# A four-layer macaron network on one core: layer 2's expert stage taken chunk by chunk, and the mixers' constants made in layer 1

## The chip, the cores and the metric

The kernel runs on one core of a Trainium2 chip. The metric is the device time of one execution in microseconds (us). A core has five engines with a queue each: TensorE (PE in the profile, with PEld for the loading of the stationary operand), VectorE (DVE), ScalarE (ACT), GpSimd (POOL) and SyncE (SP), which here only issues loads and stores. They share SBUF, of which a tile takes so many bytes in each of 128 partitions, and PSUM, eight banks into which TensorE writes.

## What is computed

The input x has 2 rows of 512 tokens with 256 features. Four layers follow, each a half-weighted feed-forward part, a mixer, and the same half-weighted feed-forward part again:

```python
x = x + 0.5 * ffn(layernorm(x))
x = x + mixer(layernorm(x))
x = x + 0.5 * ffn(layernorm(x))
```

All of it is in float32. Layer 0 has a mixture of 32 experts of which 6 are taken, around retention attention. Layer 1 has a product with a binarized weight, around attention over the most important tokens. Layer 2 has an expert stage in which the best of 8 experts is taken, around a Mamba-2 mixer with 8 heads. Layer 3 has a mixture of 8 experts of which 2 are taken, around a Mamba-2 mixer with 64 heads. The feed-forward part of layer 2, which the change rewrites, is:

```python
logits = xt @ wg                                  # xt: normalized tokens, wg: 256 x 8
probs = softmax(logits)
idx = argmax(probs)                               # the first of equal ones
gate = probs[idx]
expert_out = einsum('nh,eoh->neo', xt, W) + b     # 8 experts, 256 x 256 each
out = einsum('ne,neo->no', onehot(idx) * gate, expert_out)
```

## The kernel before

**Tiling.** The 1024 tokens lie in SBUF as 8 chunks of 128 (`self.x`, NC = 8), four (CB = 4) to a row; a chunk has its tokens on the partitions. A product over the 256 features is two matmuls of 128 (KD = 2), each of which the profile lists as two instructions. To bring the features onto the partitions, a normalized chunk is transposed on TensorE with the identity, into PSUM, and copied back by DVE or ACT.

**Order of the work.** The stages are traced in the order of `STAGES`: `l0_ffn, l0_attn, l0_ffn, l1, l2_ffn, l2_attn, l2_ffn, l3_ffn, l3_attn, l3_ffn`. Around the stages of a layer stands its `..._weights` context (L2: `l2_weights`; L3: `l3_weights`). The framework then decides the order of the instructions in each engine's queue by a planner with modelled costs: an engine takes what the plan finds ready, so that a later stage's instruction may stand before an earlier one's. In parts of the mixers the order of the queues is fixed by hand (`in_order`).

**Buffers.** SBUF and PSUM buffers come from pools that are opened and closed like brackets and laid one behind the other; a pool that is opened after another was closed takes its place. Layer 1 (`l1`) has one SBUF pool `a1` with all its buffers, PSUM pool `a1s` (banks 0 to 3: the scores), and in banks 4 to 7 first `a1m` and then `a1n`. `l2_ffn` takes all eight banks for one pool, `f2m`; the mixer of layer 2 takes all eight again (`psM` 3, `psA` 5), and so does `moe`, which layer 3 begins with.

**Layer 1's end.** `l1` has a loop of 25 steps in which, per chunk, the attention (`scores`, `turn`, `values`, `finish`, `project`) and the second feed-forward part (`front`, `turn_x`, `back`) follow each other two steps apart. The last step adds the last chunk's product to x (L1163).

**Layer 2's constants and weights.** `l2_weights` first calls `mixer_constants` for the L2 mixer: small loads of the convolution's weights and three vectors (L1537 to L1543), a memset on DVE (L1539), seven transposes (L1549, L1551) and the copies L1544 and L1552, in pools of their own that are closed at once. Then it loads the experts' weights and transposes them: 32 matmuls (L1470) in PSUM pool `f2pm` with four banks, and eight copies to `w8T`, by DVE (L130) and ACT (L132) in turn. `l3_weights` does for the L3 mixer what `mixer_constants` did for that of L2, between layer 2's second feed-forward part and layer 3.

**Layer 2's feed-forward part.** `l2_ffn` goes by whole steps over all 8 chunks: `layernorm_T` measures (L208, L209), takes the inverse deviation on POOL (L217, L218), normalizes (L223) and transposes each row (L177, copies L130 and L132) into one buffer `xT` of 8192 bytes a partition; `logits` makes the routing products of all chunks (L317, copy L320); twelve DVE and ACT instructions on 128x64 tiles give each token's weight for each expert (L1492 to L1503); `comb_transposed` transposes these (L402, two copies); and then, for each chunk, the biases' product (L1509, addition L1510) comes first, then 16 matmuls for the 8 experts (L1514), whose results DVE adds into x, weighted, one expert at a time (L1519).

**The mixer of layer 2.** `mamba` begins with a `layernorm_T` of its own: pool `xT` (8192 bytes a partition), then pool `ln`. Its first row goes through `measure` (four chunks' moments, then one pair of POOL instructions), `norm` (four times L223) and `turn` (transposes L177); then the products `pd` (L1616) and the convolutions `pp` (L1675). It reads the constants from `self.mix`.

Of the kernel before, what the change touches and what calls it, by code (L numbers as in the profile page):

```python
# [10 lines left out]
F32 = mybir.dt.float32  # L11
# [7 lines left out]
P = 128  # L19
# [64 lines left out]
class Net:  # L84
# [650 lines left out]

    @contextmanager
    def l3_weights(self):
        self.mixer_constants("L3_attn_", 64)
        yield


# [358 lines left out]
    def l1(self):  # L1100
# [18 lines left out]
        NG = NH // NQ  # L1119
        with ExitStack() as es:  # L1120
            sb = es.enter_context(tc.tile_pool(name="a1", bufs=1))
            psS = es.enter_context(tc.tile_pool(name="a1s", bufs=1, space=PSUM))

            score = psS.tile([P, NQ, 2, 2, P], F32, name="ps_s")
            wi, bq, bk, bv, bo, bi = self.l1v
            wib = sb.tile([P, KD, P], F32, name="wib")
            bqs = sb.tile([P, KD], F32, name="bqs")
            xn = sb.tile([P, NC, D], F32, name="xn")
            xT = sb.tile([P, KD, T], F32, name="xT")
            qT = sb.tile([P, KD, T], F32, name="qT")  # L1130
# [3 lines left out]
            mask = sb.tile([P, NC], F32, name="mask")  # L1134
            place = sb.tile([P, NC, P], F32, name="place")
            mx = sb.tile([P, NC, NH], F32, name="mx")
# [39 lines left out]
            def importance(b):  # L1176

                bs = slice(b * CB, (b + 1) * CB)
                pb = psM.tile([P, S], F32, tag="mm", name="pb")
                for k in range(KD):  # L1180
                    nc.tensor.matmul(
                        pb, wib[:, k, :], xT[:, k, b * S : (b + 1) * S], start=(k == 0), stop=(k == KD - 1)
                    )
                ibs[b] = sb.tile([P, S], F32, tag="ib", name="ib", bufs=2)
                nc.vector.tensor_scalar(ibs[b], pb, bi, None, ALU.add)
                own = sb.tile([P, CB, P], F32, tag="cmp", name="own", bufs=4)
                nc.vector.tensor_tensor(
                    own,
                    ibs[b].rearrange("p (c t) -> p c t", c=CB),
                    self.ident.unsqueeze(1).to_broadcast([P, CB, P]),  # L1190
                    ALU.mult,
                )
                nc.vector.tensor_reduce(imp[:, bs], own, AX.X, ALU.add)

            def ranks(b, cc):
                c = b * CB + cc
                me, ib = imp[:, c : c + 1], ibs[b]
                t = sb.tile([P, S], F32, tag="cmp", name="cmp", bufs=4)
# [4 lines left out]
                t = sb.tile([P, S], F32, tag="cmp", name="cmp2", bufs=4)  # L1203
                at = S - P - cc * P
# [36 lines left out]
            def compact(b):  # L1241
# [16 lines left out]
                xk = sb.tile([P, KD + 1, P], F32, tag="xk", name="xk", bufs=2)  # L1258
                nc.vector.tensor_copy(xk, px)
                return xk  # L1260

            def keys(b, xk):
                used = xk[:, KD, :]
                pk = psM.tile([P, KD, P], F32, tag="mm", name="pk")
                for m in range(KD):
                    for k in range(KD):
# [6 lines left out]
                        )  # L1273
                kT = sb.tile([P, KD, P], F32, tag="kT", name="kT", bufs=2)
                for m in range(KD):
# [5 lines left out]
            def vals(b, xk):  # L1281
                kept = sb.tile([P, 1], F32, tag="kept", name="kept", bufs=2)
                nc.vector.tensor_reduce(kept, xk[:, KD, :], AX.X, ALU.add)
                uc = sb.tile([P, 1], F32, tag="uc", name="uc", bufs=2)
# [4 lines left out]
                vt = sb.tile([P, D], F32, tag="vt", name="vt", bufs=2)  # L1289
                nc.vector.tensor_tensor(vt, pv, bv, ALU.add)  # L1290
                nc.vector.tensor_scalar(
                    vas[b][:, :, 0:DH], vt.rearrange("p (h d) -> p h d", h=NH), uc, None, ALU.mult
                )


            with tc.tile_pool(name="a1m", bufs=4, space=PSUM) as psM:
                for c in range(NC + 4):
                    if c < NC:
                        front(c)
                    if c == CB:  # L1300
                        wt = self.w("w4")[:, : KD * 4 * D].rearrange("p (k n d) -> p k n d", k=KD, n=4)
# [146 lines left out]
    def l2_weights(self):  # L1448
# [29 lines left out]

    def l2_ffn(self):
        nc, tc = self.nc, self.tc  # L1480
        E = 8
        with ExitStack() as es:
            psM = es.enter_context(tc.tile_pool(name="f2m", bufs=8, space=PSUM))
            xT, row, measure, norm, turn = self.layernorm_T(es, psM)
            for b in range(B):
                row(b)
            sb = es.enter_context(tc.tile_pool(name="f2", bufs=1))
            lg = self.logits(sb, psM, xT, self.wg8, E)
            m = sb.tile([P, NC], F32, name="m")
            oh = sb.tile([P, NC, E], F32, name="oh")  # L1490
            bc = m.unsqueeze(2).to_broadcast([P, NC, E])
            nc.vector.tensor_reduce(m, lg, AX.X, ALU.max)  # L1492
            nc.vector.tensor_tensor(oh, lg, bc, ALU.is_equal)
            nc.vector.tensor_tensor(lg, lg, bc, ALU.subtract)
            nc.scalar.activation(lg, lg, AF.Exp)

            nc.vector.tensor_tensor(oh, oh, self.c["desc"].unsqueeze(1).to_broadcast([P, NC, E]), ALU.mult)
            nc.vector.tensor_reduce(m, oh, AX.X, ALU.max)
            nc.vector.tensor_tensor(oh, oh, bc, ALU.is_equal)
            nc.vector.tensor_reduce(m, lg, AX.X, ALU.add)  # L1500
            nc.vector.reciprocal(m, m)
            nc.vector.tensor_tensor(lg, lg, bc, ALU.mult)
            nc.vector.scalar_tensor_tensor(lg, lg, 0.5, oh, ALU.mult, ALU.mult)  # L1503
            combT = self.comb_transposed(sb, psM, lg, 1)
            for c in range(NC):
                cs = slice(c * P, (c + 1) * P)
                xc = self.x[:, c, :]
                pb = psM.tile([P, D], F32, tag="mm", name="pb")
                nc.tensor.matmul(pb, combT[:, 0, cs], self.b8, start=True, stop=True)  # L1509
                nc.vector.tensor_tensor(xc, xc, pb, ALU.add)  # L1510
                for e2 in range(E // 2):
                    ps = psM.tile([P, 2, D], F32, tag="mm", name="ps_y")
                    for k in range(KD):
                        nc.tensor.matmul(  # L1514
                            ps, xT[:, k, cs], self.w8T[:, k, 2 * e2 : 2 * e2 + 2, :], start=(k == 0), stop=(k == KD - 1)
                        )
                    for e in range(2):
                        ei = 2 * e2 + e
                        nc.vector.scalar_tensor_tensor(  # L1519
                            xc, ps[:, e, :], lg[:, c, ei : ei + 1], xc, ALU.mult, ALU.add  # L1520
                        )


    def mixer_constants(self, pre, nh):

        nc, tc, a = self.nc, self.tc, self.a
        NX = nh * 64 // P
# [4 lines left out]
        cols = self.keep.tile([P, 7, R], F32, name=pre + "cols")  # L1534
        with tc.tile_pool(name=pre + "c", bufs=1) as sb, tc.tile_pool(name=pre + "cp", bufs=1, space=PSUM) as ps:
            cw = sb.tile([R, P, 4], F32, name="cwr")
            nc.sync.dma_start(cw, a[pre + "conv_w"].rearrange("(m p) w -> m p w", p=P))  # L1537
            v = sb.tile([R, 3, P], F32, name="vr")
            nc.vector.memset(v, 0.0)  # L1539
            nc.sync.dma_start(v[:, 0, :], a[pre + "conv_b"].rearrange("(m p) -> m p", p=P))  # L1540
            nc.sync.dma_start(v[:NX, 1, :], a[pre + "norm_w"].rearrange("(m p) -> m p", p=P))
            d = sb.tile([NX, 2], F32, name="dr")
            nc.sync.dma_start(d, a[pre + "D_param"].rearrange("(m two) -> m two", two=2))  # L1543
# [3 lines left out]
            pt = ps.tile([P, 7, R], F32, name="pt_c")  # L1547
            for w in range(4):
# [3 lines left out]
            nc.vector.tensor_copy(cols, pt)  # L1552
        self.mix = cols[:, 0:4, :], cols[:, 4, :], cols[:, 5, :], cols[:, 6, :], prm

# [7 lines left out]
    def mamba(self, pre, win, wout, nh):  # L1562
# [14 lines left out]
        with ExitStack() as es:  # L1577
# [7 lines left out]
            wb, self.wb = self.wb, None  # L1585
            cw, cb, nw, dcol, prm = self.mix
            cw = cw.rearrange("p w m -> p m w")
# [531 lines left out]
```

## Time and profile before

| | us |
|---|---|
| median of 3 runs (2030.21 to 2033.29) | 2031.36 |
| the profiled execution: its time | 2029.85 |
| its span, from first to last instruction | 2028.0 |
| PE busy | 1762.7 (87% of the span) |
| DVE busy | 1131.6 (56%) |
| POOL busy | 903.5 (45%) |
| ACT busy | 800.6 (39%) |
| granted TensorE clock, mean | 0.917 |

Times inside the profile are counted from the span's start, so 852.70 means 852.70 us after the first instruction. The profiled execution's own time is 1.85 us more than its span; the median of the runs is 1.51 us more than the profiled time. A busy PE is not a PE at its peak, because matmuls overlap: what one costs is best read from the distance between the starts of two. The granted clock is a share of full speed. In a line of the timeline the bracket at the end is the engine's idle time just before, and whose result ended it.

### The profile page before, as it was taken

The numbers are of one execution on the slowest core, as the hardware profiler recorded it, in microseconds if no ns is written. First come the engines' busy times: TensorE is split into PE (matmuls) and PEld (weight loads), VectorE is DVE, ScalarE is ACT, GpSimd is POOL, SyncE is SP. The second block draws the span as 40 slices with busy tenths as digits, with TensorE's granted clock in tenths as the row PEclk, the third lists the DMA queues.
The fourth block names the chain that finished last, engine by engine and source line by source line (L and its number), as shares of the span: only waits on it lengthen the run. The fifth ranks groups of instructions, "written<-read, shape, count | busy, mean of one in ns | idle before, by whom it ended". The sixth has DMA issues, their size and how long they took to land. (4 is left out here: it accounts for less than half of the span.)

```text
span 2028.0 us, 29711 instructions
## 1 busy us (share of the span) xinstructions
PE 1762.7 (87%) x10662; PEld 1259.7 (62%) x10662; DVE 1131.6 (56%) x2657; ACT 800.6 (39%) x1342; POOL 903.5 (45%) x889
## 2 busy tenths in 40 slices
PE   5899769888999678798788989589999899999895
PEld 4677636565777545444465367357777677777564
DVE  4533276217333476556563653578777677777443
ACT  1132224211232144301751013268777677777111
POOL 3477655311777421100240026135657456667253
PEclk8999989889999789889897979689999999999798
DMA  8266440051565500000220013434454444444133
GB/s 310 80 187 189 153 173 12 16 162 33 170 184 172 209 22 1 22 0 17 100 83 22 11 40 97 131 125 156 152 167 146 154 138 154 160 151 130 44 96 95
DMA packets 117441, 226.49 MB, mean 112 GB/s; under 512 B 22383, under 2 KB 68829, under 8 KB 117015
## 3 DMA queue, kind: packets, MB, share of 16 engines
q1 hardware_dynamic: 88134, 170.17, 26.2%
q0 software_dynamic: 20608, 48.45, 7.6%
q10 hardware_dynamic: 8528, 5.72, 0.9%
q8 instruction: 93, 1.52, 0.3%
q14 instruction: 78, 0.63, 0.1%
HBM read 195.59 MB, written 41.81 MB: 117 GB/s over the span
## 5 line engine op out<-in xcount | busy, mean ns | idle before, releaser
L527 POOL DMA_INDIRECT xe<-table,sl_get x176 | 179.9, 1022 | 202.0 <-DVE sl_get L503 148.1
L551 PE MATMUL ps_gu<-we,xeT 128*128 128x352 f32 x704 | 232.5, 472 | 0.0
L581 POOL DMA_INDIRECT rows<-ye,sl_put x176 | 177.0, 1006 | 83.7 <-issue 40.5
L1682 DVE SCALAR_TENSOR_TENSOR xc<-pp,L_attn_cols,xc 128x511 f32<-128x511 f32 (+2 forms) x216 | 161.4, 747 | 34.7 <-ACT xc L1678 29.4
L576 PE MATMUL ps_ye<-we,hT 88*128 88x256 f32 x704 | 168.3, 379 | 2.9 <-ACT ye L132 1.6
L556 DVE SCALAR_TENSOR_TENSOR he<-se,xe,ps_gu 128x176 f32<-128x176 f32 x176 | 69.9, 397 | 180.2 <-ACT se L555 169.1
L551 PEld LDWEIGHTS ps_gu<-we,xeT 128*128 128x128 f32 x704 | 130.0, 196 | 56.5 <-issue 5.5
L576 PEld LDWEIGHTS ps_ye<-we,hT 88*128 88x128 f32 x704 | 133.0, 190 | 37.0 <-ACT ye L132 3.6
L1809 PE MATMUL pz<-xT,wt 128*128 128x128 f32 x1152 | 144.4, 279 | 11.9 <-ACT xt L1758 5.5
L1785 DVE SCALAR_TENSOR_TENSOR lm<-lm,jb,top 128x128 f32<-128x128 f32 x576 | 153.6, 340 | 0.0
L1675 PE MATMUL pp<-xT,wx 128*128 128x512 f32 x288 | 144.9, 628 | 5.6 <-issue 2.4
L1809 PEld LDWEIGHTS pz<-xT,wt 128*128 128x128 f32 x1152 | 137.8, 195 | 17.0 <-issue 9.6
L1882 PE MATMUL yacc<-wt,y 128*128 128x256 f32 x576 | 144.4, 394 | 0.7 <-POOL y L1864 0.7
L1864 POOL TENSOR_TENSOR y<-y,sg 128x512 f32<-128x512 f32 x72 | 91.7, 1274 | 106.8 <-DVE y L1863 105.2
L1802 POOL TENSOR_TENSOR ce<-ce,CT 128x1024 f32<-128x1024 f32 x54 | 127.9, 2369 | 0.0
L1882 PEld LDWEIGHTS yacc<-wt,y 128*128 128x128 f32 x576 | 104.8, 191 | 24.2 <-issue 10.8
L1514 PE MATMUL ps_y<-w8T,xT 128*128 128x512 f32 x256 | 118.9, 619 | 0.0
L555 ACT ACTIVATE se<-ps_gu 128x176 f32<-128x176 f32 x176 | 55.9, 318 | 154.0 <-PE ps_gu L551 153.9
L1837 PE MATMUL py<-lm,xt 128*64 128x128 f32 x1152 | 108.0, 281 | 8.0 <-issue 6.5
L1875 POOL TENSOR_TENSOR sqs<-sqs,sq 128x512 f32<-128x512 f32 x56 | 71.4, 1275 | 89.4 <-ACT sq L1874 89.4
L1794 DVE TENSOR_TENSOR lm<-lm,M 128x1024 f32<-128x1024 f32 x72 | 87.1, 1215 | 42.7 <-ACT lm L1790 41.1
L217 POOL TENSOR_SCALAR ln_rstd<-ln_mv 128x4 f32<-128x4 f32 x15 | 3.5, 236 | 238.2 <-DVE ln_mv L209 227.5
(401 smaller groups left out, 3478.6 us busy)
## 6 DMA issues: line engine op xcount, KB each, us to landing
lm<-rows SPq DMA_DIRECT2D x72, 512.0 KB
ce<-rows SPq DMA_DIRECT2D x54, 512.0 KB
rows<-zero POOLq DMA_DIRECT2D x16, 768.0 KB, 11.8
y<-rows SPq DMA_DIRECT2D x16, 768.0 KB
we<-in_L_ffn_w_gate_dram SPq DMA_DIRECT2D x64, 176.0 KB
we<-in_L_ffn_w_up_dram SPq DMA_DIRECT2D x64, 176.0 KB
we<-in_L_ffn_w_down_dram SPq DMA_DIRECT2D x64, 176.0 KB
we<-in_L_ffn_w_dram SPq DMA_DIRECT2D x48, 176.0 KB
```

The costliest lines, as they stand in the source:

```text
L527: nc.gpsimd.indirect_dma_start(xe[:, i, :], None, table, bass.IndirectOffsetOnAxis(get[:, e * per + j : e * per + j + 1], 0), bounds_check ...
L551: nc.tensor.matmul(pg, xeT[:, k, i * P : (i + 1) * P], wgu[:, :, k], start=(k == 0), stop=(k == KD - 1))
L576: nc.tensor.matmul(py[:, i, :], hT[:, q, i * P : (i + 1) * P], wd[:, q, :], start=(q == 0), stop=(q == 1))
L581: put_rows = nc.gpsimd.indirect_dma_start(rows, bass.IndirectOffsetOnAxis(put[:, e * per + j : e * per + j + 1], 0), y[:, i, :], None, bou ...
L1514: nc.tensor.matmul(ps, xT[:, k, cs], self.w8T[:, k, 2 * e2 : 2 * e2 + 2, :], start=(k == 0), stop=(k == KD - 1))
L1675: nc.tensor.matmul(pp, wv[:, k, :], xT[:, k, b * S : (b + 1) * S], start=(k == 0), stop=(k == KD - 1))
L1682: nc.vector.scalar_tensor_tensor(out[:, 3 - w :], pp[:, : S - 3 + w], cw[:, m, w : w + 1], out[:, 3 - w :], ALU.mult, ALU.add)
L1785: nc.vector.scalar_tensor_tensor(k["lm"][:, h, :], k["lm"][:, h, :], jb[:, k["c"], n : n + 1], top, ALU.add, ALU.min)
L1802: nc.gpsimd.tensor_tensor(k["ce"], k["ce"], ct, ALU.mult)
L1809: nc.tensor.matmul(pz[:, m, :], u["wz"][:, kk, m * P : (m + 1) * P], xT[:, kk, c * P : (c + 1) * P], start=(kk == 0), stop=(kk == KD - 1),)
L1837: nc.tensor.matmul(py[i * HP : (i + 1) * HP, m, :], w[:, h * HP : (h + 1) * HP], v[:, h, :], start=(m == 0 and n == 0), stop=(n == len(src ...
L1882: nc.tensor.matmul(yacc[cc // 2][:, cc % 2, :], k["y"][:, m, :], u["wo"][:, m, :], start=(u["g"] == 0 and m == 0 and cc % 2 == 0), stop=(u ...
```

## The change

Four things are done together.

**The mixers' constants are made in layer 1.** `mixer_constants` takes the pool it is to use, issues its loads and returns a function `turn` that does the transposes and copies with a given PSUM pool. `l1` calls it for both mixers when it loads its own weights (at step CB of its first loop), and runs both `turn`s after that loop, ahead of `places(0)`, with pool `a1m`. The memset goes from DVE to POOL. `self.mix` becomes a dictionary with an entry for each mixer; `l3_weights` is gone.

**Layer 1's early buffers come first in SBUF.** The buffers that are last used in the first steps of the 25-step loop (`wib`, `xn`, `xT`, `place`, `ib`, `cmp`/`own`, `xk`, `kT`, `kept`, `uc`, `vt`) move to a pool `a1e`, which is laid ahead of `a1`.

**`l2_ffn` goes chunk by chunk.** A loop of 11 steps measures chunk s, normalizes, transposes and routes chunk s-1, makes the experts' products of chunk s-2 and adds the biases of chunk s-3. The routing's DVE instructions are on 128x8 tiles now, eight of them to a chunk, and one on ACT.

**The experts' products go ahead of the biases' product**, and the weights' transpose for the latter (`ct`) is made a chunk at a time, after the experts.

```diff
@@ l1
+            sbe = es.enter_context(tc.tile_pool(name="a1e", bufs=1))
             sb = es.enter_context(tc.tile_pool(name="a1", bufs=1))
...
-            xn = sb.tile([P, NC, D], F32, name="xn")
-            xT = sb.tile([P, KD, T], F32, name="xT")
+            xn = sbe.tile([P, NC, D], F32, name="xn")
+            xT = sbe.tile([P, KD, T], F32, name="xT")
...
                             nc.sync.dma_start(wt[:, :, n, :], a[pre + name].rearrange("(k p) d -> p k d", p=P))
+                    turns = [self.mixer_constants(p, nh, sb) for p, nh in (("L2_attn_", 8), ("L3_attn_", 64))]
...
+                for f in turns:
+                    f(psM)
                 places(0)
                 importance(1)
@@ l2_weights
-        self.mixer_constants("L2_attn_", 8)
         with tc.tile_pool(name="f2keep", bufs=1) as keep:
@@ l2_ffn
         with ExitStack() as es:
+            sb = es.enter_context(tc.tile_pool(name="f2", bufs=3))
+            st = es.enter_context(tc.tile_pool(name="f2s", bufs=1))
             psM = es.enter_context(tc.tile_pool(name="f2m", bufs=8, space=PSUM))
-            xT, row, measure, norm, turn = self.layernorm_T(es, psM)
-            for b in range(B):
-                row(b)
-            sb = es.enter_context(tc.tile_pool(name="f2", bufs=1))
-            lg = self.logits(sb, psM, xT, self.wg8, E)
...
-            combT = self.comb_transposed(sb, psM, lg, 1)
-            for c in range(NC):
...
+            ms, xts, ws = {}, {}, {}
+
+            def measure(c):
+                ms[c] = self.scale(st, c, c)
+
+            def turn(c):
+                xn = self.centre(sb.tile([P, D], F32, tag="xn", name="xn"), c, *ms.pop(c))
+                pt = psM.tile([P, KD, P], F32, tag="mm", name="pt")
+                for k in range(KD):
+                    nc.tensor.transpose(pt[:, k, :], xn[:, k * P : (k + 1) * P], self.ident)
+                xts[c] = sb.tile([P, KD, P], F32, tag="xT", name="xT")
+                nc.scalar.copy(xts[c], pt)
+
+            def route(c):
+
+                pl = psM.tile([P, E], F32, tag="mm", name="pl")
+                for k in range(KD):
+                    nc.tensor.matmul(pl, xts[c][:, k, :], self.wg8[:, k, :], start=(k == 0), stop=(k == KD - 1))
+                m, t, r = (st.tile([P, 1], F32, name=f"{n}{c}") for n in ("m", "t", "r"))
+                lg = sb.tile([P, E], F32, tag="lg", name="lg")
+                oh = sb.tile([P, E], F32, tag="oh", name="oh")
+                w = ws[c] = st.tile([P, E], F32, name=f"w{c}")
+                nc.vector.tensor_reduce(m, pl, AX.X, ALU.max)
+                nc.vector.tensor_scalar(lg, pl, m, None, ALU.subtract)
+                nc.scalar.activation(w, lg, AF.Exp)
+
+                nc.vector.scalar_tensor_tensor(oh, lg, 0.0, self.c["desc"], ALU.is_equal, ALU.mult)
+                nc.vector.tensor_reduce(t, oh, AX.X, ALU.max)
+                nc.vector.tensor_scalar(oh, oh, t, 0.5, ALU.is_equal, ALU.mult)
+                nc.vector.tensor_reduce(r, w, AX.X, ALU.add)
+                nc.vector.reciprocal(r, r)
+                nc.vector.scalar_tensor_tensor(w, w, r, oh, ALU.mult, ALU.mult)
+
+            def experts(c):
+                xT, w, xc = xts.pop(c), ws[c], self.x[:, c, :]
                 for e2 in range(E // 2):
                     ps = psM.tile([P, 2, D], F32, tag="mm", name="ps_y")
...
+            def bias(c):
+                w, xc = ws.pop(c), self.x[:, c, :]
+                ct = psM.tile([E, P], F32, tag="mm", name="ps_ct")
+                nc.tensor.transpose(ct, w, self.ident)
+                wT = sb.tile([E, P], F32, tag="wT", name="wT")
+                nc.scalar.copy(wT, ct)
+                pb = psM.tile([P, D], F32, tag="mm", name="pb")
+                nc.tensor.matmul(pb, wT, self.b8, start=True, stop=True)
+                nc.vector.tensor_tensor(xc, xc, pb, ALU.add)
+
+            for s in range(NC + 3):
+                if s < NC:
+                    measure(s)
+                if 0 <= s - 1 < NC:
+                    turn(s - 1)
+                    route(s - 1)
+                if 0 <= s - 2 < NC:
+                    experts(s - 2)
+                if 0 <= s - 3 < NC:
+                    bias(s - 3)
@@ mixer_constants
-            nc.vector.memset(v, 0.0)
+        nc.gpsimd.memset(v, 0.0)
...
-        with tc.tile_pool(name=pre + "c", bufs=1) as sb, tc.tile_pool(name=pre + "cp", bufs=1, space=PSUM) as ps:
...
+        self.mix[pre] = cols[:, 0:4, :], cols[:, 4, :], cols[:, 5, :], cols[:, 6, :], prm
+
+        def turn(psum):
...
+            pt = psum.tile([P, 7, R], F32, tag="mm", name="pt_c")
...
+        return turn
```

More of the change, by code (lines that the diff above doesn't have):

```diff
@@ L734, in l0_ffn @@
         self.moe("L0_ffn_", names, E, 176, K, 352, 4, [0, 1], 2 * (T * K // E), 8, softmax, 0.5)
[L736 to L739, printed above, removed]
     def l3_ffn(self):
@@ L1125, in l1 @@
             wi, bq, bk, bv, bo, bi = self.l1v
-            wib = sb.tile([P, KD, P], F32, name="wib")
+            wib = sbe.tile([P, KD, P], F32, name="wib")
             bqs = sb.tile([P, KD], F32, name="bqs")
-            xn = sb.tile([P, NC, D], F32, name="xn")
-            xT = sb.tile([P, KD, T], F32, name="xT")
+            xn = sbe.tile([P, NC, D], F32, name="xn")
+            xT = sbe.tile([P, KD, T], F32, name="xT")
             qT = sb.tile([P, KD, T], F32, name="qT")
@@ L1134, in l1 @@
             mask = sb.tile([P, NC], F32, name="mask")
-            place = sb.tile([P, NC, P], F32, name="place")
+            place = sbe.tile([P, NC, P], F32, name="place")
             mx = sb.tile([P, NC, NH], F32, name="mx")
@@ L1183, in importance @@
                     )
-                ibs[b] = sb.tile([P, S], F32, tag="ib", name="ib", bufs=2)
+                ibs[b] = sbe.tile([P, S], F32, tag="ib", name="ib", bufs=2)
                 nc.vector.tensor_scalar(ibs[b], pb, bi, None, ALU.add)
-                own = sb.tile([P, CB, P], F32, tag="cmp", name="own", bufs=4)
+                own = sbe.tile([P, CB, P], F32, tag="cmp", name="own", bufs=4)
                 nc.vector.tensor_tensor(
@@ L1197, in ranks @@
                 me, ib = imp[:, c : c + 1], ibs[b]
-                t = sb.tile([P, S], F32, tag="cmp", name="cmp", bufs=4)
+                t = sbe.tile([P, S], F32, tag="cmp", name="cmp", bufs=4)
                 nc.vector.tensor_scalar(t, ib, me, None, ALU.is_ge)
                 nc.scalar.activation(t, t, AF.Copy, accum_out=ge[:, c : c + 1])
-                t = sb.tile([P, S], F32, tag="cmp", name="cmp2", bufs=4)
+                t = sbe.tile([P, S], F32, tag="cmp", name="cmp2", bufs=4)
                 at = S - P - cc * P
@@ L1257, in compact @@
                     )
-                xk = sb.tile([P, KD + 1, P], F32, tag="xk", name="xk", bufs=2)
+                xk = sbe.tile([P, KD + 1, P], F32, tag="xk", name="xk", bufs=2)
                 nc.vector.tensor_copy(xk, px)
@@ L1273, in keys @@
                         )
-                kT = sb.tile([P, KD, P], F32, tag="kT", name="kT", bufs=2)
+                kT = sbe.tile([P, KD, P], F32, tag="kT", name="kT", bufs=2)
                 for m in range(KD):
@@ L1281, in vals @@
             def vals(b, xk):
-                kept = sb.tile([P, 1], F32, tag="kept", name="kept", bufs=2)
+                kept = sbe.tile([P, 1], F32, tag="kept", name="kept", bufs=2)
                 nc.vector.tensor_reduce(kept, xk[:, KD, :], AX.X, ALU.add)
-                uc = sb.tile([P, 1], F32, tag="uc", name="uc", bufs=2)
+                uc = sbe.tile([P, 1], F32, tag="uc", name="uc", bufs=2)
                 nc.vector.tensor_scalar(uc, self.c["icol"][:, 0:1], kept, None, ALU.is_lt)
@@ L1288, in vals @@
                     nc.tensor.matmul(pv, xk[:, k, :], wt[:, k, 2, :], start=(k == 0), stop=(k == KD - 1))
-                vt = sb.tile([P, D], F32, tag="vt", name="vt", bufs=2)
+                vt = sbe.tile([P, D], F32, tag="vt", name="vt", bufs=2)
                 nc.vector.tensor_tensor(vt, pv, bv, ALU.add)
@@ L1489, in l2_ffn @@
[L1489 to L1503, printed above, removed]
-            combT = self.comb_transposed(sb, psM, lg, 1)
-            for c in range(NC):
[L1506 to L1510, printed above, removed]
+            ms, xts, ws = {}, {}, {}
@@ L1514, in l2_ffn @@
                         nc.tensor.matmul(
-                            ps, xT[:, k, cs], self.w8T[:, k, 2 * e2 : 2 * e2 + 2, :], start=(k == 0), stop=(k == KD - 1)
+                            ps, xT[:, k, :], self.w8T[:, k, 2 * e2 : 2 * e2 + 2, :], start=(k == 0), stop=(k == KD - 1)
                         )
@@ L1518, in l2_ffn, with mixer_constants @@
                         ei = 2 * e2 + e
[L1519 to L1528, printed above, removed]
+                        nc.vector.scalar_tensor_tensor(xc, ps[:, e, :], w[:, ei : ei + 1], xc, ALU.mult, ALU.add)
+            def bias(c):
[17 more added lines that the diff above has]
+                    bias(s - 3)
+    mix = {}
+    def mixer_constants(self, pre, nh, sb):
+        nc, a = self.nc, self.a
         NX = nh * 64 // P
@@ L1534, in mixer_constants @@
         cols = self.keep.tile([P, 7, R], F32, name=pre + "cols")
-        with tc.tile_pool(name=pre + "c", bufs=1) as sb, tc.tile_pool(name=pre + "cp", bufs=1, space=PSUM) as ps:
-            cw = sb.tile([R, P, 4], F32, name="cwr")
-            nc.sync.dma_start(cw, a[pre + "conv_w"].rearrange("(m p) w -> m p w", p=P))
-            v = sb.tile([R, 3, P], F32, name="vr")
-            nc.vector.memset(v, 0.0)
[L1540 to L1543, printed above, removed]
+        cw = sb.tile([R, P, 4], F32, name=pre + "cwr")
+        nc.sync.dma_start(cw, a[pre + "conv_w"].rearrange("(m p) w -> m p w", p=P))
+        v = sb.tile([R, 3, P], F32, name=pre + "vr")
+        nc.gpsimd.memset(v, 0.0)
+        nc.sync.dma_start(v[:, 0, :], a[pre + "conv_b"].rearrange("(m p) -> m p", p=P))
+        nc.sync.dma_start(v[:NX, 1, :], a[pre + "norm_w"].rearrange("(m p) -> m p", p=P))
+        d = sb.tile([NX, 2], F32, name=pre + "dr")
+        nc.sync.dma_start(d, a[pre + "D_param"].rearrange("(m two) -> m two", two=2))
+        self.mix[pre] = cols[:, 0:4, :], cols[:, 4, :], cols[:, 5, :], cols[:, 6, :], prm
+        def turn(psum):
             nc.vector.tensor_copy(
@@ L1546, in mixer_constants @@
             )
-            pt = ps.tile([P, 7, R], F32, name="pt_c")
+            pt = psum.tile([P, 7, R], F32, tag="mm", name="pt_c")
             for w in range(4):
@@ L1552, in mixer_constants @@
             nc.vector.tensor_copy(cols, pt)
-        self.mix = cols[:, 0:4, :], cols[:, 4, :], cols[:, 5, :], cols[:, 6, :], prm
+        return turn
     wb = None
@@ L1585, in mamba @@
             wb, self.wb = self.wb, None
-            cw, cb, nw, dcol, prm = self.mix
+            cw, cb, nw, dcol, prm = self.mix[pre]
             cw = cw.rearrange("p w m -> p m w")
```

## The prediction

> **What bounds the kernel now.** The page's chain of waits reaches only the end of layer 3, so I read the stages around the change instead: first busy time by window, then the timeline at the windows' edges, then SyncE's waits. Columns: length, then busy time (and instructions) of PE, PEld, DVE, ACT, POOL, then the granted clock.
>
> ```profile
> 820.00:832.00 12.00, 10.08 (x86) 6.20 (x86) 8.98 (x14) 6.64 (x13) 1.52 (x3) 1.00 0.01 1
> ...
> 846.00:852.70 6.70, 4.84 (x10) 2.64 (x10) 0.84 (x2) 0.62 (x2) 0.00 (x0) 0.51 0.00 0
> 852.70:879.40 26.70, 17.90 (x97) 15.32 (x97) 13.59 (x46) 4.35 (x8) 2.62 (x4) 0.63 0.13 41
> 879.40:943.50 64.10, 63.10 (x143) 26.50 (x142) 37.20 (x84) 0.00 (x0) 1.27 (x2) 0.97 0.00 0
> 1082.00:1100.20 18.20, 13.31 (x58) 11.26 (x58) 7.17 (x26) 3.29 (x5) 1.26 (x2) 0.50 0.00 0
> 1100.20:1165.00 64.80, 63.64 (x143) 26.69 (x142) 39.21 (x91) 0.00 (x0) 1.27 (x2) 0.96 0.03 9
> ```
>
> While the experts run (rows 4 and 6) TensorE is the bound: 98% busy. Ahead of them lies a lead-in of 26.7 us in the first feed-forward part and of 18.2 us in the second, in which TensorE is busy 67% and 73% at a low clock. The last steps of layer 1 (rows 1 and 2) leave TensorE idle too.
>
> ```profile
> 852.28 0.42 DVE L1163 TENSOR_TENSOR x<-x,ps_y 128x256 f32<-128x256 f32 x1 [3.44 <-PE ps_y L1162]
> ...
> 857.84 6.34 PE L1470 MATMUL ps_w<-cst,w 128*128 128x128 f32 x32 [2.11 <-DVE L_attn_cols L1552]
> ...
> 870.08 3.58 PE L317 MATMUL ps_lg<-wg,xT 128*128 128x8 f32 x16 [0.68 <-DVE xT L130]
> ...
> 876.20 0.22 DVE L1503 SCALAR_TENSOR_TENSOR lg<-lg,oh 128x64 f32<-128x64 f32 x1
> ...
> 879.42 9.26 PE L1514 MATMUL ps_y<-w8T,xT 128*128 128x512 f32 x16
> ...
> 896.93 7.13 PE L1514 MATMUL ps_y<-w8T,xT 128*128 128x512 f32 x16
> 904.62 7.13 PE L1514 MATMUL ps_y<-w8T,xT 128*128 128x512 f32 x16
> ...
> 943.69 1.07 PE L177 MATMUL ps_tr<-cst,xn 128*128 128x128 f32 x8 [1.19 <-DVE x L1519]
> ```
>
> The lead-in is a chain of whole steps: layer 1 ends at 852.70; the convolution's constants (until 857.84); the experts' weights (6.34); all transposes and logits (until 873.66); the routing on DVE (until 876.42); its transposes and first biases; the first experts at 879.42. They end at 942.50, and 1.19 us later the mixer's transposes start, since its norm was made beside the experts. The mixer's last addition ends at 1081.89; the second part has the same chain, without the constants and weights: first experts 1100.24, x final at 1165.04.
>
> ```profile
> 852.25 0.29 SPq L1537 DMA_DIRECT2D cwr<-in_L_attn_conv_w_dram  x1
> ```
>
> This load is issued at 852.25, just after layer 1's last matmul (852.18), though the place it goes to was last read near 771: a new pool waits for the whole of the pool it lies on. By that rule I judge the moves.
>
> **The Trainium skill.** Its page "TensorE: Matmul & The Clock Gate", section "What's actually happening", says that TensorE runs at half clock until it has been busy some 3.4 us and falls back after as long an idle time. The trace agrees: the clock is 0.51 in 879.4 to 883.8 and 1.00 in 883.8 to 888, which is why the first chunk takes 9.26 us and a later one 7.13. Section "Part 4: PE-mode transpose" of the same page says that transposes don't count as busy for this. The trace disagrees: within the weights' transposes the clock goes from 0.50 (857.8 to 861.3) through 0.72 to 1.00 (864.8 to 869.5). So weights transposed early help the clock. "VectorE: DVE Perf Modes", section "The TRN2 errata — SBUF-src ops pay a fixed extra latency per instruction", says that small tiles pay their latency each time. The trace agrees: the reciprocal on 128x8 takes 0.20 us, the routing on 128x64 0.22. A routing cut into eight costs eight times as much.
>
> **The change, part by part.** All sums are against the profiled execution: span 2028.0, time 2029.85. The median is 2031.36, 1.51 above that.
>
> *A feed-forward stage after the change*, as TensorE's work. Chunks' pitch is now 7.69 us (896.93 to 904.62): 16 matmul pairs at 0.429 and a biases' product of 0.83. Eight chunks: 61.5. Transposes and logits, 48 instructions at 0.114 (24 took 2.74 from 866.66): 5.5. The eight transposes of ct at 0.15: 1.2. Changes between groups of small and large matmuls, three a chunk, which the trace of before shows only at the biases (about 0.4) and in layer 1's loop (about 0.1): I take 0.15 each, 3.6, with ends 0 and 9.6. Sum 71.8. To this come the fill, from the first transpose to the first logits, 0.8; half clock at the start, 2.7 (9.26 and, in the second part, 9.78 against 7.13 for the first experts, and a little on the transposes); waits of TensorE on DVE or on a PSUM bank, 0.2 a chunk, 1.6 (ends 0 and 8: nothing in the trace has this mix). The last chunk's biases, 1.0, come after the last experts. So the last experts end 71.8 + 0.8 + 2.7 + 1.6 − 1.0 = 75.9 after the start.
>
> What of DVE lies beside this: per chunk eight additions L1519 at about 0.515 (4.1), statistics 0.66, norm 0.45, routing eight at 0.23 (1.8), biases 0.45: 7.5 against TensorE's 9.0. I cost it at nothing; rival E says what if this cover is gone.
>
> *First part.* The convolution's constants leave (852.70 to 857.84). The weights' buffers, f2keep (17,472 bytes a partition), lie on the place of `a1e`, whose last reader runs at 783.0, so the loads come early. Their PSUM pool f2pm lies on the scores' banks, last read at 831.74. So the 32 transposes run in layer 1's tail, where TensorE is idle 21 − 14.3 = 6.7 us of 831.7 to 852.7; they need 6.34, some of it at half clock, in the order the planner likes. Chunks 0 to 6 can be measured and normalized in that tail as well, as f2 and f2s also fit on `a1e`; f2m takes all banks and waits for layer 1's last read. So the stage starts at 852.70 and its last experts end at 928.6, against 942.50: **−13.9**.
>
> *Its exit.* f2s begins 7,872 bytes past f2keep and is 1,792 long; the mixer's transposed row is 8,192 long and its `ln` pool follows. So f2s and `ln` overlap, and the mixer's measuring, today hidden beside the experts, waits for the biases of the last chunk. Four statistics 2.2 (948.14 to 950.35 for the same), POOL's pair 1.35 (950.44 to 951.80), four norms 1.4, and the biases of 1 + 0.45 ahead of them: the transposes end 7.1 after the last experts, against 2.3 now (944.76): +4.9. In those 7 us the clock falls; the products after them, some 6 us at full, lose about 1.5. **+6.4**, bounds 0 (the pool rule doesn't bite) and +8. Net of the first part: **−7.5**.
>
> *Second part.* No weights here; f2s waits for the mixer's row, last used at 1069.4, before 1081.9, so no new wait. Start 1082.0, an ACT table load (1.28 in this mixer, partly seen) 0.5, 75.9: last experts at 1158.4. Then ct, its copy, biases and addition, 2.1: x is final at 1160.5, against 1165.04: **−4.5**.
>
> *Layer 3's front.* Its constants stood between: the load waited 3.6 us, and row 0's transposes, whose norm was ready before, waited behind them. With the constants gone row 0's eight (1.84 for half of the 3.67) go ahead: **−2.0** (−4 if the router's load also moves ahead, 0 if row 1's norm sets the pace).
>
> *Layer 1.* The constants of both mixers: two loads of the convolution's weights and three vectors each on SP, early among loads that have time; a memset on POOL, whose queue is idle there; 14 transposes, about 2 us, where TensorE is idle for 5.04 us at 733.21; four DVE copies, 1.2 us, where DVE is busy 18.0 of 23.0 us: **+0.8** (0 to 2). The weights' transposes and eight copies (0.6 to 0.7 each) among layer 1's last chunks: **+1.0** (−2, the clock kept up, to +6, all exposed).
>
> Sum: −7.5 − 4.5 − 2.0 + 0.8 + 1.0 = −12.2. Span 2015.8, time 2017.65, as a median **2019.2**.
>
> **Rivals.** *B, more is gained*: the mixer's norm isn't delayed (−6.4), and the early weights keep the clock up into the first part (−2.1): 2010.7. For: each needs only a different layout or order than I worked out. Against: the byte count above. 18%. *C, the weights don't get ahead of layer 1's end* (the change doesn't do what it says): the 6.34 come after 852.70 and save the 1.0: 2024.5. For: the planner may put layer 1's own work first. Against: 21 us with idle TensorE. 10%. *D, the stage's eight tiles a chunk* (five before) *wait for PSUM banks*: 0.75 more a chunk, sixteen chunks, +12: 2031.2, no change. 11%. *E, slower: DVE's queue becomes the bound.* DVE takes its instructions in order; if the routing's round trips stand in it (exp on ACT 0.5, POOL's pair 1.1, the transposed copy and the logits 1.6), a chunk takes 7.5 + 3.2 = 10.7 in place of 9.0: +27.7, 2046.9. It eats the gain from 0.76 a chunk (9.7 us), and is slower by more than 0.2% from a chunk of 10.0. For: the trace of before gives 0.71 of DVE's idle time per pair of additions, so there is little slack. Against: the planner can put the next chunks' steps a chunk ahead. 9%. My own case: 52%.
>
> **How the numbers follow.** 0.2%, 4 us, is about what a measurement of this kernel can tell from no change. B with layer 1 at no cost and the front at −4 gives 2006.9; D gives 2031.2. The range 2007 to 2031 leaves out about half of D, E and a little of B: below 2 in 10. Faster: my case, B and C, 0.80, less 0.04 of my case that ends near no change: 0.76. Same: D and that, 0.15. Slower: E, 0.09.
>
> **What would show it.** Right: L1470's transposes between 832 and 853; first experts by 857; chunks' starts 8.8 to 9.3 apart; the last experts near 928; then a gap of 6 to 7 us with `ln_st` after x's last addition; layer 3's row 0 transposed ahead of row 1. B: the mixer's `ln_st` among the experts. C: L1470 after 852. D: TensorE's waits end on releases of banks. E: chunks over 9.7 apart, DVE over 90% busy or waiting on ACT and POOL while TensorE waits on it. I am wrong if layer 1's loop itself becomes longer by more than 3 us, or if the stages outside these windows change.

## The result and the profile after

The changed kernel takes 2049.31 us (median of 4 runs, 2045.93 to 2052.91), the kernel before 2031.45 beside it: a ratio of 1.0087, 95% interval 1.0069 to 1.0106. I had forecast 2019.2. Its profiled span is 2047.6 us. Most of what was lost was lost in a place where I had expected next to nothing, layer 1.

One sentence ahead of this document's prediction is wrong. It says that `mixer_constants` is called at step CB of layer 1's first loop. In the diff the line `turns = [...]` stands one level further out than the loads above it: it is in the body of the loop, not under `if c == CB`, and so the constants of both mixers are loaded in **each of the 12 steps**, 24 sets in place of two. I built layer 1's term on the wrong reading.

Lines of the changed kernel's timeline, SyncE's queue first, then TensorE:

```profile
679.89 1.97 SPq L701 DMA_DIRECT2D y<-rows  x4
682.34 0.29 SPq L1568 DMA_DIRECT2D L_attn_cwr<-in_L_attn_conv_w_dram  x1
...
709.57 2.00 SPq L701 DMA_DIRECT2D y<-rows  x4
711.61 0.86 SPq L1300 DMA_DIRECT2D w<-in_L_attn_Wq_dram  x1
...
716.33 4.37 PE L707 MATMUL ps_add<-y,cst 128*128 128x256 f32 x12 [14.22 <-DMA y<-rows]
...
759.42 0.61 PE L1583 MATMUL pt_c<-cst,L_attn_cwr 6*128 6x6 f32 x4 [7.17 <-DMA L_attn_cwr<-in_L_attn_conv_w_dram]
...
776.28 0.71 PE L1344 MATMUL ps_s<-kb,qT 32*128 32x256 f32 x8
```

Layer 0's expert outputs for x's second row are loaded at L701. In the kernel before all eight loads were issued together, at 676.69. Now four are, and the other four stand behind 32 loads of constants (eight sets of the four loads shown at L1568 to L1574) until 709.57; TensorE waits 14.22 us for them. The attention's weights come after that. The last sets of constants land only by 759 and 762, and TensorE waits 7.17 us for the first of them at the head of the work that leads to the scores. From the first addition (684.00 before, 687.09 now) to the first scores (748.24, 776.28) it is 64.24 us before and 89.19 after, 25.0 more. The span grew by 19.6, so all the rest together gained about 5.

SyncE's queue between 676 and 768, by what it waited for (in all, times, longest):

```profile
SPq L1571 <- POOL L_attn_vr L1570: 15.8, 9, 3.4
SPq L1571 <- POOL ln_rs L193: 7.3, 2, 5.3
SPq L1574 <- DMA y<-rows: 3.3, 2, 1.7
```

All 12 sets of one mixer go to the same buffers. So a memset on POOL waits until that mixer's set before has landed, the load of the bias waits for its memset, and POOL's queue has layer 1's own norms in it. Of the 27 us that the 32 loads took between 682.34 and 709.57, 9.9 are their own issue times, 9.6 are waits for the memset, and 6.1 are waits that the profile puts down to the first four output loads (`y<-rows`); the loads behind the outputs wait for these in the kernel before too.

The stages of layer 2 that answer to the windows shown of before (length, then busy time and instructions of PE, PEld, DVE, ACT and POOL, then the granted clock, the share of DMA and GB/s):

```profile
846.00:881.62 35.62, 30.04 (x218) 19.90 (x217) 21.21 (x48) 13.87 (x26) 9.97 (x22) 0.95 0.00 1
881.62:884.92 3.30, 2.28 (x13) 1.73 (x13) 1.85 (x9) 0.85 (x3) 0.79 (x2) 0.75 0.81 264
884.92:963.96 79.04, 72.52 (x189) 32.23 (x189) 45.03 (x138) 5.72 (x21) 0.00 (x0) 0.95 0.01 3
1107.28:1111.47 4.19, 3.08 (x12) 2.31 (x13) 2.55 (x13) 1.66 (x3) 2.43 (x6) 0.50 0.01 2
1111.47:1189.88 78.41, 71.89 (x189) 32.08 (x189) 48.55 (x157) 6.31 (x23) 2.48 (x5) 0.95 0.02 7
```

Layer 1's tail keeps TensorE busy 84% now, with the experts' weights in it. The lead-ins have shrunk from 26.7 and 18.2 us to 3.3 and 4.2; the stages with the experts have grown from 64.1 and 64.8 to 79.0 and 78.4. TensorE is busy 92% in them, no longer 98%. DVE, rival E's suspect, is busy 57% and 62%. Why they grew shows at a chunk's end (timeline, TensorE):

```profile
895.76 7.11 PE L1525 MATMUL ps_y<-w8T,xT 128*128 128x512 f32 x16
902.71 0.27 PE L1535 MATMUL ps_ct<-cst,w 128*8 128x128 f32 x1
903.32 0.69 PE L1539 MATMUL pb<-b,wT 8*128 8x256 f32 x2 [0.34 <-ACT wT L1537]
903.95 0.44 PE L1496 MATMUL pt<-cst,xn 128*128 128x128 f32 x2
904.90 0.61 PE L1504 MATMUL pl<-wg,xT 128*128 128x8 f32 x4 [0.52 <-ACT xT L1498]
905.37 7.11 PE L1525 MATMUL ps_y<-w8T,xT 128*128 128x512 f32 x16
...
934.26 8.81 PE L1525 MATMUL ps_y<-w8T,xT 128*128 128x512 f32 x16
```

All small products of two chunks stand in a row between two blocks of experts. Two of them need what the one just before has made, by way of a copy on ACT, and TensorE waits 0.34 and 0.52 us. A chunk takes 9.61 us. And one chunk of each stage, here that of 934.26, takes 8.81 us for its experts in place of 7.11: a part of it ran at a lower clock (granted 0.57 and 0.52 from 934.26 to 938, 1.00 from there on).

The way out of the first part (timeline):

```profile
965.76 0.23 POOL L217 TENSOR_SCALAR ln_rstd<-ln_mv 128x4 f32<-128x4 f32 x1 [82.15 <-DVE ln_mv L209]
...
967.72 2.21 PE L177 MATMUL ps_tr<-cst,xn 128*128 128x128 f32 x8 [4.21 <-DVE xn L223]
...
973.74 6.22 PE L1710 MATMUL pp<-xT,wb 128*128 128x512 f32 x8
```

The mixer's norm is on the path, as worked out from the byte counts. The last experts end at 961.0, the transposes at 969.9, and the mixer's first products (3.68 us for eight before, at a clock of 1.00) run at half clock until 978.

### The profile page after: what moved, and what is told of

It is laid out like the page before. It is cut to its first block, busy times and chain, and to the rows that moved or that the text cites. A ratio compares the mean times of both kernels' runs of the same rounds, so it can differ in the third digit from the quotient of the medians.

```text
span 2047.6 us, 30151 instructions
## 1 busy us (share of the span) xinstructions
PE 1760.2 (86%) x10662; PEld 1255.6 (61%) x10662; DVE 1142.5 (56%) x2755; ACT 808.8 (39%) x1382; POOL 920.7 (45%) x937
## 5 line engine op out<-in xcount | busy, mean ns | idle before, releaser
L1917 PEld LDWEIGHTS yacc<-wt,y 128*128 128x128 f32 x576 | 105.0, 192 | 25.4 <-issue 10.4
L1860 POOL TENSOR_TENSOR xd<-xt,dec 128x512 f32<-128x512 f32 x54 | 56.3, 1043 | 103.3 <-ACT xt L1793 103.3
```

Source lines behind the costliest of these rows:

```text
L1917: nc.tensor.matmul(yacc[cc // 2][:, cc % 2, :], k["y"][:, m, :], u["wo"][:, m, :], start=(u["g"] == 0 and m == 0 and cc % 2 == 0), stop=(u ...
```

## The experiments

Each ran beside the kernel before on the same chip, and only the ratio to it counts (its 95% interval in brackets): the times of the kernel before lie between 2022 and 2037 us there. The parts below are read from the profiles, one execution of each kernel. The time up to layer 1's first addition scatters between 682 and 689 us among all these kernels with no order in it, and what follows layer 3's front between 844 and 850; neither is put down to an edit. From layer 1's first scores to its end it is 103.7 to 109.0 us in the seven kernels whose code is the same there, so a difference of a few us in that section alone shows nothing.

**Call once.**

```diff
                         for n, name in enumerate(("Wq", "Wk", "Wv", "Wo")):
                             nc.sync.dma_start(wt[:, :, n, :], ...)
-                    turns = [self.mixer_constants(p, nh, sb) for ...]
+                        turns = [self.mixer_constants(p, nh, sb) for ...]
```

> The changed kernel, with the call of mixer_constants moved under the test for step CB, so that the constants are loaded once instead of in each of the loop's 12 steps. Theory 'repeated loads' (24 sets of loads stand on SyncE's queue ahead of the second row's expert outputs and of the attention's weights): the scores of layer 1 start 28 us earlier, 2049.3 - 28 = 2021. Rival 'place' (constants made in layer 1 cost there even if made once): scores at most 10 us earlier, about 2040.

2026.08, ratio 0.9989 (0.9977 to 1.0002). The eight loads of L701 are together again, and the constants' transposes wait for nothing:

```profile
681.52 4.39 SPq L701 DMA_DIRECT2D y<-rows  x8
...
738.78 0.64 PE L1583 MATMUL pt_c<-cst,L_attn_cwr 6*128 6x6 f32 x4
...
753.73 0.71 PE L1344 MATMUL ps_s<-kb,qT 32*128 32x256 f32 x8
```

First addition to first scores: 65.04, which is 24.15 less than in the changed kernel and 0.8 more than before. "Repeated loads" holds in this section (24 of the 28 us) and "place" falls. But the total is 5 us above the 2021 expected: the change as I had read it is worth 2 us and not 12, and the interval does not even rule out none.

**The constants' part alone, in 12 steps and in one** (the kernel before, with the changed `mixer_constants` and nothing else).

> The kernel before, with only the constants' part of the change, call in all 12 steps as in the changed kernel. Theory 'repeated loads': +28 in layers 0 and 1, -5.1 in the first feed-forward part of layer 2 (852.70 to 857.84 go), -2 at layer 3's front: 2031.5 + 21 = 2052. Rival 'layout' (layer 1 is held up by the early buffers' own pool and the weights' early loads, not by the constants): 2031.5 - 7 = 2025.

> The kernel before, with only the constants' part of the change, call in one step alone. Theory 'repeated loads': 2031.5 - 5.1 - 2 + 1 = 2025. Rival 'place': layer 1's first loop stays longer by 10 to 20, 2034 to 2044.

2052.77, ratio 1.0112 (1.0092 to 1.0133), and 2032.55, ratio 1.0007 (0.9993 to 1.0021). First addition to scores: 89.28 and 64.76. So the 24.5 us come with the repeated loads, without the new layout or chunks: "layout" falls as well, and so does "place". Both expectations were right on that and wrong on a second point; that the first one's total of 2052 was met is luck, since it counted on gains in layer 2 that did not come. Taken alone, the constants made once show no gain: from layer 1's end to the first experts it is 28.00 us, where it was 26.72. Their loads and transposes, and the weights' transposes held up behind them, had hidden the statistics, POOL's pair and the norms of both rows. Without them TensorE waits for these instead (timeline of the kernel with one call):

```profile
863.58 1.94 PE L177 MATMUL ps_tr<-cst,xn 128*128 128x128 f32 x8 [4.45 <-DVE xn L223]
...
868.66 0.69 PE L177 MATMUL ps_tr<-cst,xn 128*128 128x128 f32 x2 [3.14 <-DVE xn L223]
```

The first line is x's first row, the second the second.

**14 sets, none ahead of the outputs** (`if c > CB:` ahead of the changed kernel's call).

> The changed kernel with the call in the 7 steps after step CB, so still 14 sets of loads, but none ahead of the second row's expert outputs. Theory 'queue' (the harm is what waits behind the loads on SyncE: 14.2 us for the second row's outputs, 7.2 for the last set of constants): the first loop of layer 1, from its first addition to the first scores, goes from 89 to 65 to 72 us, total 2026 to 2033. Rival 'amount' (each set costs about 1 us wherever it stands, by SyncE's and POOL's time): 7/12 of the 24 us stay, 79 us, total 2040.

2031.63, ratio 1.0017 (1.0005 to 1.0028). First addition to scores 69.26: "queue" holds, "amount" (79) falls. With 7/12 of the sets left, 4.2 of the 24 us are left, and these are seen in TensorE's waits for the last sets:

```profile
735.38 0.61 PE L1584 MATMUL pt_c<-cst,L_attn_cwr 6*128 6x6 f32 x4 [1.88 <-DMA L_attn_cwr<-in_L_attn_conv_w_dram]
737.62 0.27 PE L1586 MATMUL pt_c<-cst,L_attn_vr 6*128 6x6 f32 x1 [1.28 <-DVE L_attn_vr L1579]
738.73 0.69 PE L1584 MATMUL pt_c<-cst,L_attn_cwr 34*128 34x34 f32 x4 [0.84 <-DMA L_attn_cwr<-in_L_attn_conv_w_dram]
```

**Layout without chunks** (constants once, the pool `a1e`, the feed-forward part in whole steps).

> The kernel before with the constants made once in layer 1 and layer 1's early buffers in a pool of their own, the feed-forward part still in whole steps. Theory 'layout' (what the first feed-forward part won in the changed kernel comes from weights and norms made early, not from chunks): from layer 1's end to the last experts 78 to 82 us, against 91.8 with the constants alone and 78.0 to 79.4 with chunks; total 2020. Rival 'chunks' (the chunk loop makes the gain): 86 or more; total 2028.

2023.46, ratio 0.9978 (0.9964 to 0.9991). Its experts' weights and first transposes on TensorE:

```profile
850.71 0.38 PE L1469 MATMUL ps_w<-cst,w 128*128 128x128 f32 x2
...
860.21 1.97 PE L177 MATMUL ps_tr<-cst,xn 128*128 128x128 f32 x8 [0.58 <-DVE x L1160]
```

Layer 1's end (860.15) to the last experts: 81.27 us, against 91.75 with the constants alone and 78.03 with chunks. "Layout" holds: 10.5 of the 13.7 us are early weights (32 transposes done by 851, before layer 1's end) and early norms, 3.2 are chunks. The second part, where there is nothing to make early, takes 83.09 without chunks and 82.6 to 86.0 with them. Against the 3.2 us stands the way out: from the last experts to the mixer's end it is 143.2 us here and 146.7 in the call once. So in its own order the loop over chunks shows no gain: the ratio without it is 0.9978, with it 0.9989, and the intervals overlap.

**A gap ahead of f2 and f2s**, on top of the call once:

```diff
+            es.enter_context(tc.tile_pool(name="f2gap", bufs=1)).tile([P, 13 * 256], F32, name="gap")
             sb = es.enter_context(tc.tile_pool(name="f2", bufs=3))
```

> The first of these kernels with an unused pool of 13,312 bytes ahead of f2 and f2s, so that neither lies on the mixer's row or ln pool. Theory 'pool': the mixer's statistics of row 0 move among the experts and its transposes follow the last biases at once: 6 to 7 us less than the first kernel, about 2015. Rival 'order' (the planner puts the mixer's statistics last whatever the layout): as the first kernel, about 2021.

2021.05, ratio 0.9961 (0.9944 to 0.9977). "Pool" holds: the mixer's statistics (L208) lie among the experts now, and the transposes follow the last addition at once:

```profile
898.45 0.43 DVE L208 BATCH_NORM_STATS2 ln_st<-x 128x6 f32<-128x256 f32 x1
...
938.26 0.42 DVE L1541 TENSOR_TENSOR x<-x,pb 128x256 f32<-128x256 f32 x1 [0.88 <-PE pb L1540]
938.74 1.29 PE L177 MATMUL ps_tr<-cst,xn 128*128 128x128 f32 x8 [0.52 <-DVE x L1541]
...
943.76 6.64 PE L1711 MATMUL pp<-xT,wb 128*128 128x512 f32 x8
```

From the last experts to these products it is 8.04 us, against 12.74 in the call once; the products themselves are still slow (6.64 us), and of 4.7 us 2.7 are left at the mixer's end. The median is 5.0 us below the call once, where 6 to 7 were expected.

**Small products woven in** (with the gap). `experts` runs one function ahead of each of its four pairs, under `in_order` for PE: transposes of chunk c+1 and of the weights of chunk c-1 ahead of the second pair, logits of c+1 ahead of the third, biases of c-1 ahead of the fourth.

```diff
                 for e2 in range(E // 2):
+                    for f, i in between:
+                        if i == e2:
+                            f()
                     ps = psM.tile([P, 2, D], F32, tag="mm", name="ps_y")
```

> Constants once, the gap of the fourth kernel, and the small products of a chunk put by hand between the experts' products of another: transposes of chunk c+1 and of the weights of chunk c-1 after the first pair of experts, logits of c+1 after the second, biases of c-1 after the third. Theory 'boundary' (TensorE waits at each chunk's end on ACT's copies, and the clock falls there now and then): chunks 8.3 to 8.6 apart in place of 9.61, none of 8.8 us length; both stages 8 to 12 us shorter, total about 2003. Rival 'work' (the small products' own changes of operand take the time wherever they stand): chunks stay at 9.3 or more, total about 2018.

1999.27, ratio 0.9862 (0.9837 to 0.9886). "Boundary" holds:

```profile
873.21 0.38 PE L1497 MATMUL pt<-cst,xn 128*128 128x128 f32 x2
873.43 0.27 PE L1540 MATMUL ps_ct<-cst,w 128*8 128x128 f32 x1
873.54 1.88 PE L1529 MATMUL ps_y<-w8T,xT 128*128 128x512 f32 x4
875.25 0.51 PE L1505 MATMUL pl<-wg,xT 128*128 128x8 f32 x4
875.62 1.96 PE L1529 MATMUL ps_y<-w8T,xT 128*128 128x512 f32 x4
877.51 0.69 PE L1547 MATMUL pb<-b,wT 8*128 8x256 f32 x2
878.14 3.70 PE L1529 MATMUL ps_y<-w8T,xT 128*128 128x512 f32 x8
881.67 0.38 PE L1497 MATMUL pt<-cst,xn 128*128 128x128 f32 x2
```

The same products with no wait listed: a chunk takes 881.67 - 873.21 = 8.46 us. The two parts take 67.84 and 72.30 us, against 79.37 and 83.55 with the gap alone.

**The woven kernel with the constants left where the kernel before makes them.**

> The last kernel with the mixers' constants made where the kernel before makes them. Theory 'constants matter' : the 5.1 and 2 us of the prediction come back at layer 2's beginning and at layer 3's front, 7 above the last kernel. Rival 'hidden' (with the early pool their loads and transposes fit in layer 1's tail as well, and only layer 3's front pays): 0 to 3 above it.

2002.28, ratio 0.9888 (0.9857 to 0.9918). The medians are 3 us apart and the intervals overlap. In the profiles the first part is 1.7 us longer than in the woven kernel (69.52) and layer 3's front, from x final to its first large products (L365), 1.9 shorter (11.84 against 13.77). Both go with the clock: the first experts begin at 0.52 here and at 1.00 in the woven kernel, while from layer 1's end to their start it is 1.5 us in both; and the router's 32 products of layer 3 take 4.09 us at 0.88 here, 6.83 at 0.50 there. That speaks against 5.1 us in layer 2, as "hidden" has it; at layer 3's front the wait for the constants' load (3.74 us) is back, but the clock covers what it costs. Whether the constants' part is worth anything in all isn't settled.

**Fillers in the waits at a chunk's end** (the kernel with the gap, useless transposes of the identity, and the order of TensorE's queue fixed by hand).

> The fourth kernel (constants once, gap, chunks in the changed kernel's order) with useless transposes of the identity in the two waits of each chunk's end: four after the transposes, ahead of the logits, three after the weights' transpose, ahead of the biases; about 0.11 us each, so that they fit in waits of 0.52 and 0.40 us. Theory 'idle' (the chunks of 8.8 us are a fall of the clock that these waits bring about): no chunk of 8.8 us in either stage, chunks 9.6 to 9.8 apart, first to last expert 73 to 75 us in both stages where the fourth kernel has 75.7 and 76.4. Rival 'load' (the clock is cut now and then however TensorE is kept busy): one to three chunks of 8.8 us in each stage as before, 75 to 79 us.

2032.24, ratio 1.0018 (1.0005 to 1.0032). Inconclusive. The fillers took more than the waits (chunks 10.4 apart), and one chunk of the second stage still has the low clock:

```profile
1103.57 8.80 PE L1528 MATMUL ps_y<-w8T,xT 128*128 128x512 f32 x16
```

One in 16, against two in 16 in the kernel with the gap, is no difference to build on. The Trainium skill ("TensorE: Matmul & The Clock Gate", "Part 4: PE-mode transpose") says that transposes don't count as busy for the clock; by that these fillers were the wrong ones. But in the kernel before, the clock rose from 0.50 to 1.00 within the weights' transposes, as the prediction read, and the measurement decides. Matmuls in their place were not tried.

**Biases among the chunk's own experts**, on the woven kernel (`d = s - 2` in place of `s - 3`).

> The seventh kernel with each chunk's biases among its own experts in place of those of the next chunk. If TensorE's slack after the last experts causes the half clock of the mixer's first products (6.5 us for the eight that took 3.7 before), then x is final 0.6 us earlier in each stage, the mixer's first products take 3.7 to 4 us, and the whole is 3 to 5 us shorter than the seventh kernel, about 1995. Rival: the products are slow for another reason, and it is 1 us shorter, 1998.

1995.52, ratio 0.9834 (0.9818 to 0.9851), the best of all; its interval overlaps that of the woven kernel. TensorE's idle time ahead of the mixer's transposes is 1.19 us again, as before the change, x is final 1.04 us after the second part's last experts (1.66), and yet the mixer's first products take 5.99 us. So the longer slack after the last experts is not what slows them. The total expected, 1995, was met all the same, by luck: the step that was to bring it did not come. Nor do the chunks slow them, as the layout without chunks shows:

```profile
942.61 1.06 PE L177 MATMUL ps_tr<-cst,xn 128*128 128x128 f32 x8 [1.19 <-DVE x L1518]
...
947.16 5.84 PE L1678 MATMUL pp<-xT,wb 128*128 128x512 f32 x8
```

The two kernels with the constants alone have 5.75 and 5.92 us. There TensorE does the same instructions after the same waits as in the kernel before, and only in the profile of the latter does the clock stay at 1.00. What lowers it is open.

## Why the prediction was wrong

By its own terms, in us of the profiled spans (first to last, the same sections in each profile, against the kernel before):

| term | forecast | changed kernel | call once |
|---|---|---|---|
| layer 1, first addition to x final | +1.8 | +25.8 | 0.0 |
| first part, to the last experts | −13.9 | −10.4 | −11.8 |
| exit and mixer | +6.4 | +6.9 | +7.3 |
| second part | −4.5 | −0.6 | +2.8 |
| layer 3's front | −2.0 | −0.9 | −0.9 |
| what lies before and after these | 0 | −1.2 | +1.5 |
| sum | −12.2 | +19.6 | −1.1 |

**The step that failed** is "Layer 1. The constants of both mixers: two loads of the convolution's weights and three vectors each on SP, early among loads that have time". There were 24 sets and not two, and they had no time: they stood ahead of the second row's expert outputs. Cost forecast 0.8 us, measured 24.2 more than with one call (changed kernel against call once) and 24.5 (constants alone, 12 steps against one). I counted the instructions of one call correctly and did not count the calls, though the indentation in the diff shows them. And even then I named no neighbour on SP's queue: had I listed what is behind the loads, L701 would have been the first entry.

**The second part** and a piece of the first were mis-sized, above all by one term: "waits of TensorE on DVE or on a PSUM bank, 0.2 a chunk". A chunk's pitch was to be 8.97 plus 0.2 of waits; it is 9.61, with 0.86 of waits, on ACT's copies. I priced each small product and took for granted that the planner would set them among the experts. It set them in a row, each behind the copy that it needs. The woven kernel's 8.46 lies below my 8.97, and even below the 8.53 that are left of it without any price for the changes of operand: these and the small products were priced too high. To the waits comes the clock in mid-stage, which I had at nothing: 1.7 us for each chunk that it hits, one or two in a stage, and three in the second part of the first experiment, which is why that part got longer.

**What held**: the weights' transposes ran in layer 1's tail, between 863 and 876, and rival C falls; layer 1's loop from the scores on took 105.3 us against 104.5, where I had said +1.0, though this lies within the scatter of that section.

**The exit** was right in its mechanism and met its number by luck. The mixer's norm was held back, as the pool rule had it, and the gap set it free. But the three kernels with whole steps, in which nothing is held back, also have 3.8 us more than the kernel before from the last experts to the mixer's end, with the slow first products. So of the 7 us only about 3 to 3.5 go with the chunks and the pools (2.7 by the gap, 3.5 against the layout without chunks), where I had 4.9 for the delay; the rest goes mostly with the clock, for which I had 1.5 and which falls without the delay too.

**The rivals.** Rival D came nearest in kind for the chunks, but for waits on copies and not on banks. Rival E gave 2046.9, close to the result by chance alone: its chunks of 10.7 us and full DVE are not there.

Not tried: the experts ahead of the biases, by itself; in the woven kernels the question has no meaning. Open: what lowers the clock within a stage when small products stand in a row (9 of 48 chunks in the profiles of the changed kernel, the call once and the gap, cold first chunks not counted as low; none of 48 in the three woven ones). No wait of TensorE inside these stages is longer than 0.52 us, far less than the idle time that the prediction took to be needed for a fall of the clock. Open too is what holds it down in the mixer's first products.

## What to carry to other kernels

Read a moved call's indentation and multiply: so many instructions of one call times so many calls, and then write down what stands behind them on each queue, above all the loads whose data somebody is waiting for. A loop over chunks removes a lead-in but puts its small dependent products between the large ones; in this kernel it paid only once each of them had a large product between itself and the copy that it needs. And a step that seems to stand on the path may only be hiding the next one: taking the constants away alone showed no gain.

## What the runs showed of the hardware

Small loads of repeated sets into the same buffers, with a memset in each set that waits for the set before, went through SyncE's queue at 27 us for 32, nearly three times their issue times, and the loads behind them waited too (TensorE got its operands 14.22 us late). In the changed kernel, where TensorE was busy 92% in the experts' stages with waits of 0.34 to 0.52 us in each chunk, the experts' products ran at a lower clock for a part of a chunk now and then (8.8 us in place of 7.1). In the three woven kernels, with no wait listed in the middle of these stages, none did. And the same instructions after the same 1.19 us wait ran once at a clock of 1.00 (3.68 us for the mixer's first eight products) and three times at about half (5.75 to 5.92).
